# A megakernel's middle stage: a second kind of turn for the chains up to routing, and linear attention's chains at another distance

## The chip, the cores and the metric

The kernel runs on one core of one Trainium2 chip, in one launch. The metric is the device time in microseconds (us) from the first to the last instruction of that core, as a median of several runs. A profiled execution is a further run, with the hardware profiler on; its rows are what the text works with.

## The reference, cut to what matters

Four layers, each an attention and a feed-forward part, follow one another on x of 8 batches x 512 rows x 128 columns in float32. Each part's output is normalised and added to x (the residual). The parts that matter here lie in the middle:

```
L0 attention, L0 mixing                     per batch
L1 attention: a small network learnt step by step over the batches (state handed on from batch to batch),
              then served on each batch
L1 feed-forward: softmax over 8 experts; each row goes to its best expert;
              pos = (cumsum(oh, axis=0) * oh).sum(-1) - 1;  keep = pos < capacity
              y = relu(x @ w1[e] + b1[e]) @ w2[e] + b2[e] for kept rows, x itself for the others
L2 attention: linear attention, softplus of normalised q and k, per batch
L2 feed-forward: every expert picks its best rows over ALL batches, then computes
L3 attention, L3 feed-forward
```

Row positions in the L1 experts are counted over all rows in order, so the batches are routed one after another. The L2 experts choose over all 4096 rows, so they can't begin before the last batch has been through the linear attention and its router.

## The kernel before, in words

The kernel is written with generators. A *chain* is a Python generator that emits some instructions for the engines and then yields; whoever steps the chains sets the order in which instructions stand in the five engines' queues. Each engine works off its own queue in that order.

Stage "first" (L0 attention) is dense and carries the early batches of the other chains in its background. When it ends, `l0` returns the chains that are not finished (`bg.first`). In the built program these are six: `Learn.serve_chain` and `Learn.chain` (at batch 5), `Mix.chain` (batch 6), `Learn.prepare` (batch 6), the residuals of L0 attention (batch 7) and `Route.chain` (the end of batch 4). They are called the *first chains* below: all the work up to routing. The residual of batch 7 feeds mixing of batch 7, that feeds preparing, learning, serving and at last routing of batch 7.

Stage "between" is the stage of this change. An object `Rounds` holds a list of chains, and `turn()` steps every chain once, in the order of the list. Besides the first chains it holds:

- `Passes.chain` (L1 experts). `PASSES = (5, 8)`: pass 1 runs when five batches are routed and takes their rows, pass 2 when all eight are and takes the rows of batches 5 to 7. `once()` runs one pass: four expert inputs are loaded, then a loop over e = 0..9 does `taken(e)` (two transposes on TensorE and a copy on VectorE), `given(e-2)` (16 matmul passes for the second layer, an add on VectorE, a store, and the fetch of a later expert's two weight tiles of 256 KB) and `hidden(e-1)` (8 matmul passes for the first layer, two evictions on ScalarE and two on VectorE), and yields once per e.
- `Pairs.chain`, which adds one `Pairs.batch(b)` per batch: the linear attention chain, with the gather of the L1 experts' results ahead of it and the L2 router behind. It waits until the pass that the batch belongs to is done, adds the chain of a batch, and lets five turns go by before the next (L1256). `Pairs.batch` has 29 steps, most of them one instruction group on one engine: a normalisation is a step of statistics (VectorE, then a power on GpSimd, L194), a step of scaling (ScalarE, four instructions at L217) and a step of adding to x (GpSimd); it has four of them, a query-key-value product (L1311), square, logarithm and exponentials (L1317 to L1339), a product of keys and values (L1342), the output (L1358) and the router (L1399).

`tile_sandwich_kernel` turns the rounds until all eight batches are routed (`route.done`). Then it gives the first chains' memory back and builds `Experts` (the L2 experts), which issues nine loads from SyncE's queue (one of 16 KB that the next line's transposes read, L179, six of 256 KB, two small ones), a further one of 512 KB, and 4 small transposes on TensorE. After that it turns until no chain is left. The stage that follows begins with `l2f_turn_ps` (L1497), which reads the scores of all batches.

A count of the yields gives 92 turns for the stage. Pass 1 is loaded in turn 4 and worked in turns 5 to 14; batch 0 of the linear attention begins in turn 17 and the others at a distance of five turns; routing ends in turn 42; pass 2 is loaded in turn 42 and worked in turns 43 to 52 beside batches 0 to 4; batch 5 begins in turn 54, batch 7 ends in turn 92.

Of the kernel before, what the change touches and what calls it, by code (L numbers as in the profile page):

```python
# [18 lines left out]
B = 8  # L19
# [29 lines left out]
PASSES = (5, B)  # L49
# [21 lines left out]
class Ctx:  # L71


    def __init__(self, es: ExitStack, tc: tile.TileContext, consts: bass.AP):
        self.tc = tc
        nc = self.nc = tc.nc
        pool = lambda name, bufs, **kw: es.enter_context(tc.tile_pool(name=name, bufs=bufs, **kw))
        self.keep = pool("keep", 1)
        self.shared = pool("shared", 2)
        self.dram = pool("dram", 1, space=DRAM)  # L80

        self.c = self.keep.tile([P, C_ALL], F32, name="consts_sb", tag="consts_sb")
        nc.sync.dma_start(self.c, consts)
        self.ident = self.c[:, C_ID : C_ID + P]
        self.triu = self.c[:, C_TRIU : C_TRIU + P]
        self.ones = self.keep.tile([P, P], F32, name="ones", tag="ones")
        nc.vector.memset(self.ones, 1.0)
        self.mhalf = self.keep.tile([P, 8], F32, name="mhalf", tag="mhalf")
        nc.vector.memset(self.mhalf, -0.5)
        self.x = [self.keep.tile([P, NJ, D], F32, name=f"x{b}", tag=f"x{b}") for b in range(B)]  # L90

        self.home = self.keep

        self.ps = pool("ps", 1, space=PSUM)
        self.turn = [0]
        es.enter_context(tc.manual_schedule())

        self.brisk = False
# [154 lines left out]
class Background:  # L253
# [29 lines left out]
    def turn(self, gen):  # L283

        self.first.remove(gen)
        self.first.append(gen)
        self.step(self.first, gen)
# [801 lines left out]
class Passes:  # L1089
# [37 lines left out]
    def once(self, base, rows, results):  # L1127
        cx, nc = self.cx, self.cx.nc
        NF = self.NF
        cap, ns = CAP1, CAP1 // P  # L1130
        of_expert = lambda t, e: t[e * cap : (e + 1) * cap, :].rearrange("(s p) d -> p s d", p=P)
        loads, xts, hts = {}, {}, {}

        def load(e):
            if e < NE:
                loads[e] = cx.work([P, ns, D], "l1f_xg", bufs=4)
                nc.sync.dma_start(loads[e], of_expert(rows, e))

        def taken(e):
            xg = loads.pop(e)  # L1140
            t = cx.bank("l1f_xT_ps")
            for s in range(ns):
                nc.tensor.transpose(t[:, s * P : (s + 1) * P], xg[:, s, :], cx.ident)
            xts[e] = cx.work([D, cap], "l1f_xT")
            nc.vector.tensor_copy(xts[e], t[:, :cap])
            load(e + 4)

        def hidden(e):
            hts[e] = cx.work([P, NF, cap], "l1f_hT")
            xt = xts.pop(e)  # L1150
            for f2 in range(NF // 2):
                hp = cx.bank("l1f_h_ps")
                for i in range(2):
                    f = 2 * f2 + i
                    nc.tensor.matmul(  # L1155
                        hp[:, i * cap : (i + 1) * cap],
                        self.ws[base + e][0][:, f * P : (f + 1) * P],
                        xt,
                        start=True,
                        stop=True,  # L1160
                    )
                for i in range(2):
                    f = 2 * f2 + i
                    src, bias = hp[:, i * cap : (i + 1) * cap], self.b1c[:, f, e : e + 1]
                    if i == 0:
                        nc.scalar.activation(hts[e][:, f, :], src, AF.Relu, bias=bias)
                    else:
                        nc.vector.tensor_scalar(hts[e][:, f, :], src, bias, 0.0, ALU.add, ALU.max)

        def given(e):  # L1170
            ht = hts.pop(e)
            w2 = self.ws.pop(base + e)[1]
            yp = cx.bank("l1f_y_ps")
            for s in range(ns):
                ss = slice(s * P, (s + 1) * P)
                for f in range(NF):
                    nc.tensor.matmul(yp[:, ss], ht[:, f, ss], w2[:, f, :], start=(f == 0), stop=(f == NF - 1))  # L1177
            y = cx.work([P, ns, D], "l1f_y")
            nc.vector.tensor_add(
                y,  # L1180
                yp[:, :cap].rearrange("p (s d) -> p s d", d=D),
                self.b2b[:, e * D : (e + 1) * D].unsqueeze(1).to_broadcast([P, ns, D]),
            )
            nc.sync.dma_start(of_expert(results, e), y)
            self.weights(base + e + 3)

        for e in range(4):
            load(e)
        yield
        for e in range(NE + 2):  # L1190
            if e < NE:
                taken(e)
            if e >= 2:
                given(e - 2)
            if 1 <= e <= NE:
                hidden(e - 1)
            yield


class Rounds:  # L1200


    def __init__(self, chains):
        self.chains = list(chains)

    def add(self, chain):
        self.chains.append(chain)

    def turn(self):
        for chain in list(self.chains):  # L1210
            try:
                next(chain)
            except StopIteration:
                self.chains.remove(chain)


class Pairs:
# [23 lines left out]
    def chain(self, passes, mix, rounds):  # L1241

        cx = self.cx
        for _ in range(3):
            yield
        self.w, self.gw = (
            cx.transposed(w, n, raw=raw) for w, n, raw in zip(self.args, ("w2a", "w2f_gate"), self.raws)
        )
        while not mix.over:
            yield  # L1250
        cx.nc.scalar.preload_act_table_set("natural_log_exp_and_others")
        for b in range(B):
            while passes.done <= self.route.turn(b):
                yield
            rounds.add(self.batch(b))
            for _ in range(5 if b + 1 < B else 0):  # L1256
                yield

    def batch(self, b):
        cx, nc, route = self.cx, self.cx.nc, self.route  # L1260
# [696 lines left out]
@with_exitstack  # L1957
def kernel(ctx: ExitStack, tc: tile.TileContext, a: dict, out: bass.AP):
    cx = Ctx(ctx, tc, a["consts"])
    nc = tc.nc  # L1960
    for b in range(B):
        nc.sync.dma_start(cx.x[b], a["L0_attn_x"][b].rearrange("(j p) d -> p j d", p=P))
    of = lambda layer, *names: [a[f"{layer}_{n}"] for n in names]
    route = Route(cx, *of("L1_ffn", "w_switch", "b_switch"))
    right = ExitStack()
    with cx.phase("first"):
        cx.w = right.enter_context(tc.tile_pool(name="chains", bufs=2, side="right"))
        with cx.beside("attention") as ca:
            mix = Mix(cx, *of("L0_ffn", "W_r", "W_k", "W_v", "mu_r", "mu_k"))
            learn = Learn(cx, route, *of("L1_attn", "t_k", "t_v", "t_q", "W1", "b1", "W2", "b2"))  # L1970
            chains = l0(cx, Attention(ca), *of("L0_attn", "Wq", "Wk", "Wv"), mix, learn)

        cx.brisk = True
        with cx.beside("between") as cb:
            rounds = Rounds(chains)
            passes = Passes(cb, route, *of("L1_ffn", "w1", "b1", "w2", "b2"))
            pairs = Pairs(cb, route, *of("L2_attn", "W_qkv"), *of("L2_ffn", "gate_w"))
            rounds.add(passes.chain())
            rounds.add(pairs.chain(passes, mix, rounds))
            while route.done < B:  # L1980
                rounds.turn()
            right.close()
            ce = right.enter_context(cx.beside("experts", side="right"))
            experts = Experts(ce, pairs, *of("L2_ffn", "ln_w", "ln_b", "fc1s", "b1s", "fc2s", "b2s"))
            while rounds.chains:
                rounds.turn()
    cx.brisk = False
    with cx.phase("last"):
        at = Attention(cx)
        ffn = L3Ffn(cx, *of("L3_ffn", "W1", "b1", "W2", "b2", "Wu", "bu"), out)  # L1990
        with cx.beside("staging") as cs:
            cs.home = cx.home
            weights = l3_weights(cs, *of("L3_attn", "Wqkv", "bqkv", "Wout", "bout"))
            ffn.load()
            weights = experts.run(cs, weights)
        right.close()
        cx.w = right.enter_context(tc.tile_pool(name="tiles", bufs=2, side="right"))
        with right:
            l3(cx, at, experts, ffn, weights)
# [62 lines left out]
```

## Time and profile before

| what | value |
|---|---|
| time, median of 3 runs | 2128.79 us (2126.2 to 2131.81) |
| the profiled execution's own time | 2132.52 us |
| its span, first to last instruction | 2130.7 us |
| TensorE matmul busy over the span | 1772.0 us, 83% |
| VectorE / ScalarE / GpSimd busy | 1290.8 / 1085.9 / 500.2 us |
| granted TensorE clock, mean | 0.871 |
| stage "between": first instruction of turn 1, last of turn 92 | 750.5 us, 1122.8 us |
| routing's scatters to the experts' rows (L1067), 32 of them: first and last start | 347.9 us, 951.1 us |

Busy is the time in which an engine worked on an instruction; a matmul in float32 shows as two records and overlaps its neighbours, so that a busy TensorE is not TensorE at its peak. The granted clock is the share of TensorE's full clock that its throttle let through in the stretch asked for. Idle time of an engine is put down to what ended it.

### The profile page before, as it was taken

The numbers are of one execution on the slowest core, as the hardware profiler recorded it, in microseconds if no ns is written. First come the engines' busy times: TensorE is split into PE (matmuls) and PEld (weight loads), VectorE is DVE, ScalarE is ACT, GpSimd is POOL, SyncE is SP. The second block draws the span as 40 slices with busy tenths as digits, with TensorE's granted clock in tenths as the row PEclk, the third lists the DMA queues.
The fourth block names the chain that finished last, engine by engine and source line by source line (L and its number), as shares of the span: only waits on it lengthen the run. The fifth ranks groups of instructions, "written<-read, shape, count | busy, mean of one in ns | idle before, by whom it ended". The sixth has DMA issues, their size and how long they took to land.

```text
span 2130.7 us, 31833 instructions
## 1 busy us (share of the span) xinstructions
PE 1772.0 (83%) x10886; PEld 1012.4 (48%) x10886; DVE 1290.8 (61%) x4012; ACT 1085.9 (51%) x2272; POOL 500.2 (23%) x566
## 2 busy tenths in 40 slices
PE   3999999898989967649446773799999999999996
PEld 1444545454534456437335552444554454545454
DVE  2777786777777665546447422777666666665522
ACT  1566655555554732346552221366666565665653
POOL 1001111112121122442523485222212121110001
PEclk7999988899988887659565786799999999999998
DMA  5212101011100032016214132111101010100000
GB/s 127 39 33 39 34 16 38 14 39 22 32 16 15 14 104 83 23 27 180 79 50 124 24 42 36 31 32 29 27 9 31 11 27 12 29 12 6 9 6 10
DMA packets 198064, 81.83 MB, mean 38 GB/s; under 512 B 97604, under 2 KB 189674, under 8 KB 197904
## 3 DMA queue, kind: packets, MB, share of 16 engines
q1 hardware_dynamic: 190224, 73.61, 14.3%
q0 software_dynamic: 7680, 6.19, 1.9%
q8 instruction: 87, 1.43, 0.3%
q14 instruction: 73, 0.60, 0.1%
HBM read 45.25 MB, written 31.59 MB: 36 GB/s over the span
## 4 chain that ended last, share of the span: by engine, by line
PE 55%; DVE 23%; ACT 6%; issue 6%; POOL 5%; DMA 3%; SPq 2%; POOLq 0%; ACTq 0%; DVEq 0%
PE at_o L411 11%; PE at_s L393 11%; DVE at_mx L394 8%; PE at_st L400 6%; PE l3f_y_ps L1930 5%; PE l3f_h_ps L1923 5%; DVE ln_st L203 2%; PE flip L239 2%; POOL l2f_out L1686 2%; POOL ln_rs L194 1%; PE l1f_h_ps L1155 1%; PE l1f_y_ps L1177 1%; POOL l2f_xg L1081 1%; PE at_ops L425 1%; DVE ln_mv L205 1%
## 5 line engine op out<-in xcount | busy, mean ns | idle before, releaser
L394 DVE TENSOR_REDUCE at_mx<-at_s 128x1 f32<-128x512 f32 x1024 | 642.3, 681 | 302.3 <-PE at_st L400 233.9
L393 PE MATMUL at_s<-qk 32*128 32x512 f32 x2048 | 612.0, 655 | 35.6 <-DMA qk<-qk_zero 21.3
L403 ACT ACTIVATE at_e<-at_st 128x512 f32<-128x512 f32 x1024 | 535.7, 597 | 193.6 <-PE at_st L400 152.4
L400 PE MATMUL at_st<-qk 32*128 32x512 f32 x2048 | 610.2, 655 | 18.4 <-DVE at_mx L394 12.6
L194 POOL TENSOR_TENSOR ln_rs<-ln_ve,mhalf 128x4 f32<-128x4 f32 x136 | 138.3, 1017 | 837.5 <-DVE ln_ve L188 773.7
L393 PEld LDWEIGHTS at_s<-qk 32*128 32x128 f32 x2048 | 232.2, 194 | 177.4 <-issue 57.7
L400 PEld LDWEIGHTS at_st<-qk 32*128 32x128 f32 x2048 | 240.5, 192 | 111.7 <-issue 41.8
L411 PE MATMUL at_o<-at_e,pad_v 128*32 128x512 f32 x2048 | 254.2, 641 | 14.8 <-DVE at_mx L394 14.8
L411 PEld LDWEIGHTS at_o<-at_e,pad_v 128*32 128x32 f32 x2048 | 66.9, 117 | 197.5 <-issue 173.8
L1930 PEld LDWEIGHTS l3f_y_ps<-w3f,l3f_hT 128*128 128x128 f32 x1024 | 131.8, 197 | 46.3 <-issue 26.8
L1930 PE MATMUL l3f_y_ps<-w3f,l3f_hT 128*128 128x128 f32 x1024 | 136.9, 282 | 3.2 <-ACT l3f_hT L1924 2.0
L419 ACT COPY at_ot<-at_o 128x512 f32<-128x512 f32 x64 | 37.5, 585 | 199.5 <-PE at_o L411 199.5
L1923 PE MATMUL l3f_h_ps<-l3f_xT,w3f 128*128 128x512 f32 x256 | 131.2, 611 | 0.0
L1924 ACT ACTIVATE l3f_hT<-l3f_h_ps,w3f_b1c 128x512 f32<-128x512 f32 x128 | 85.0, 683 | 64.1 <-PE l3f_h_ps L1923 64.0
L1933 DVE SCALAR_TENSOR_TENSOR l3f_o<-l3f_y_ps,l3f_w,l3f_o 128x128 f32<-128x128 f32 x128 | 44.4, 348 | 93.3 <-PE l3f_y_ps L1930 93.1
L217 ACT ACTIVATE l_xn<-x,ln_off,ln_rs 128x128 f32<-128x128 f32 x96 | 39.5, 482 | 81.5 <-DVE ln_off L211 75.4
L239 PE MATMUL flip<-consts_sb,l_xn 128*128 128x128 f32 x96 | 29.6, 398 | 54.4 <-ACT l_xn L217 54.1
L203 DVE BATCH_NORM_STATS2 ln_st<-x 128x6 f32<-128x128 f32 x256 | 55.2, 278 | 18.2 <-POOL x L937 12.4
L1686 POOL DMA_INDIRECT l2f_out<-l2f_y,l2f_idx x32 | 50.5, 1579 | 21.9 <-DVE l2f_y L1683 13.1
L1923 PEld LDWEIGHTS l3f_h_ps<-l3f_xT,w3f 128*128 128x128 f32 x256 | 42.2, 194 | 23.9 <-issue 10.0
L1773 POOL TENSOR_TENSOR l_qk<-l_r,consts_sb 128x256 f32<-128x256 f32 x32 | 21.9, 686 | 133.2 <-DVE l_r L1768 133.2
L366 POOL COPY pad_v<-l_in 128x128 f32<-128x128 f32 x32 | 9.4, 294 | 185.4 <-DMA l_in<-l_v 147.9
(412 smaller groups left out, 2551.0 us busy)
## 6 DMA issues: line engine op xcount, KB each, us to landing
l1f_w<-in_L_ffn_w SPq DMA_DIRECT2D x32, 256.0 KB
l2f_parts<-l2f_out SPq DMA_DIRECT2D x32, 256.0 KB
l2f_out<-l1f_zero SPq DMA_DIRECT2D x24, 256.0 KB
l_qk<-l_qkT SPq DMA_DIRECT2D x16, 256.0 KB
qk<-l_qk SPq DMA_DIRECT2D x128, 32.0 KB
qk<-at_mt SPq DMA_DIRECT2D x256, 2.0 KB
qk<-l_qkT SPq DMA_DIRECT2D x128, 32.0 KB
l2f_x<-l2f_rows SPq DMA_DIRECT2D x8, 272.0 KB
```

The costliest lines, as they stand in the source:

```text
L194: self.nc.gpsimd.tensor_tensor(rs, ve, self.mhalf[:, :NJ], ALU.pow)
L203: nc.vector.bn_stats(st[:, j, :], src[:, j, :])
L239: self.nc.tensor.transpose(t[:, j * P : (j + 1) * P], src[:, j, :], self.ident)
L393: nc.tensor.matmul(s, qk[:, 0, c * P : (c + 1) * P], qk[:, 1, :], start=True, stop=True)
L394: nc.vector.tensor_reduce(mx[n][:, c, h : h + 1], s, AX.X, ALU.max, negate=True)
L400: nc.tensor.matmul(s, qk[:, 1, c * P : (c + 1) * P], qk[:, 0, :], start=True, stop=True)
L403: nc.scalar.activation(es[g][:, h, :], s, AF.Exp, scale=scale)
L411: nc.tensor.matmul(o[32 * h : 32 * h + 32, :], vp[:, c, h, :], e[:, h, :], start=(c == 0), stop=(c == NJ - 1),)
L1686: nc.gpsimd.indirect_dma_start(out=self.pairs.summed[s], out_offset=bass.IndirectOffsetOnAxis(ap=idx[e][:, s : s + 1], axis=0), in_=ys[e][ ...
L1923: nc.tensor.matmul(hp, self.w1[:, e, f * P : (f + 1) * P], xt, start=True, stop=True)
L1924: nc.scalar.activation(hts[e][:, f], hp, AF.Relu, bias=self.b1c[:, f, e : e + 1])
L1930: nc.tensor.matmul(yp[:, :D], hts[e][:, f, js], self.w2[:, e, f, :], start=(f == 0), stop=(f == NF - 1))
```

## The change

Three things are changed in the stage "between".

`Rounds` has two lists, `first` (the first chains) and `chains` (all others). One turn goes through `chains`, and ahead of each of them it steps every chain of `first` once. While there are two others, the first chains thus take two steps in a turn.

`Passes.once` yields three times instead of once after its loads, and, while not all batches are routed, once more between `given` and `hidden`.

`Pairs.chain` lets four turns go by between the chains of batches 0 to 4 and the next, and three after batches 5 and 6, where it was five.

```
-        yield
+        for _ in range(3):
+            yield
         for e in range(NE + 2):
             if e < NE:
                 taken(e)
             if e >= 2:
                 given(e - 2)
+
+            if self.route.done < B:
+                yield
             if 1 <= e <= NE:
                 hidden(e - 1)
             yield
...
-    def __init__(self, chains):
-        self.chains = list(chains)
+    def __init__(self, first):
+        self.first = list(first)
+        self.chains = []
...
+    def step(self, queue, chain):
+        try:
+            next(chain)
+        except StopIteration:
+            queue.remove(chain)
+
     def turn(self):
-        for chain in list(self.chains):
-            try:
-                next(chain)
-            except StopIteration:
-                self.chains.remove(chain)
+        for other in list(self.chains) or [None]:
+            for chain in list(self.first):
+                self.step(self.first, chain)
+            if other is not None:
+                self.step(self.chains, other)
+
+    @property
+    def over(self):
+        return not self.first and not self.chains
...
             rounds.add(self.batch(b))
-            for _ in range(5 if b + 1 < B else 0):
-                yield
+            if b + 1 < B:
+                for _ in range(4 if b < PASSES[0] else 3):
+                    yield
...
-            while rounds.chains:
+            while not rounds.over:
                 rounds.turn()
```

The instructions themselves and their number are those of before; only their order in the queues differs. A count of the yields of the changed kernel gives 80 turns: the first chains take their 42 steps in turns 1 to 21, pass 1 is loaded in turn 4 and worked in turns 7 to 24, `Experts` is built after turn 21, pass 2 is loaded in turn 25 and worked in turns 28 to 37, batches 0 to 7 of the linear attention begin in turns 26, 30, 34, 38, 42, 46, 49 and 52, and batch 7 ends in turn 80.

## The prediction

> **What bounds the kernel now.** I read three views of the profile: the busy time by stretch, the waits by stretch, and the page's costliest groups. The change touches nothing outside the stage "between" (750.5 to 1122.8 us, 372.3 us of a span of 2130.7), so that stage alone is priced. Its stretches are turns 1 to 16 (pass 1), 17 to 41 (first chains and batches 0 to 4), the pause around the last scatter, turns 43 to 52 (pass 2 with batches 0 to 4) and turns 53 to 92 (the other batches):
>
> ```profile
> 750.00:842.00 92.00, 65.73 (x412) 56.55 (x412) 52.27 (x205) 27.52 (x63) 20.41 (x24) 0.85 0.36 105
> 842.00:951.00 109.00, 65.69 (x242) 47.21 (x241) 57.90 (x292) 44.66 (x100) 52.44 (x49) 0.61 0.07 21
> 951.00:960.00 9.00, 1.34 (x8) 1.35 (x9) 5.14 (x25) 2.11 (x5) 4.07 (x4) 0.50 0.42 123
> 960.00:1010.00 50.00, 46.10 (x297) 40.00 (x295) 32.32 (x139) 33.14 (x74) 10.88 (x10) 0.98 0.58 172
> 1010.00:1123.00 113.00, 55.51 (x185) 36.93 (x184) 52.27 (x281) 61.23 (x135) 44.07 (x41) 0.59 0.27 76
> ```
>
> The columns are length, TensorE, its weight loads, VectorE, ScalarE, GpSimd (each with its count), granted clock, DMA share, GB/s. Only 960 to 1010 has a full engine (TensorE, 46 of 50 us). Elsewhere no engine is over 75% busy: the time is latency, handed from engine to engine. The waits say so, here VectorE, ScalarE and GpSimd waiting for each other in the last stretch (total us, times, longest):
>
> ```profile
> POOL ln_rs L194 <- DVE ln_ve L188: 36.7, 11, 6.0
> ACT l_xn L217 <- DVE ln_off L211: 17.8, 7, 4.7
> DVE l2a_m L1347 <- PE l2a_kv_ps L1342: 16.8, 4, 4.8
> ```
>
> In the late part of pass 1 (798 to 842) TensorE's queue stands for a first chain's VectorE work, with the expert's matmuls queued behind it; and at 951 it stands for a load that `Experts` issues:
>
> ```profile
> PE l0f_k_ps L668 <- DVE ln_off L211: 7.2, 1, 7.2
> ...
> PE col L179 <- DMA raw_b<-in_L_ffn_b1s: 8.1, 1, 8.1
> ```
>
> **How I price turns.** The steps of a turn fall to different chains, so they can run side by side as far as engines differ. For each turn I add up, engine by engine, the measured durations of the steps in it, and take the fullest engine; summed over turns this is a floor that only overlap across turns can undercut. Against the present trace the floor is 49.0 us for turns 43 to 52 (took 50.3, factor 1.03, five batches and a pass in flight), 34.5 for turns 17 to 26 (took 32.0 with ScalarE's last piece, factor 0.93), 31.6 for turns 35 to 41 (took 40.7, factor 1.29) and 100.6 for turns 53 to 92 (took 113.1, factor 1.12, mostly two to four batches in flight). The main durations, from the page and from the view of one tile:
>
> ```profile
> L194 POOL TENSOR_TENSOR ln_rs<-ln_ve,mhalf 128x4 f32<-128x4 f32 x136 | 138.3, 1017 | 837.5 <-DVE ln_ve L188 773.7
> L203 DVE BATCH_NORM_STATS2 ln_st<-x 128x6 f32<-128x128 f32 x256 | 55.2, 278 | 18.2 <-POOL x L937 12.4
> L217 ACT ACTIVATE l_xn<-x,ln_off,ln_rs 128x128 f32<-128x128 f32 x96 | 39.5, 482 | 81.5 <-DVE ln_off L211 75.4
> L1317 ACT ACTIVATE l2a_sq<-l2a_qkv x8: 1056/1060/1062, 891.2 to 1084.8; 128x1024 f32<-128x1024 f32 x8
> ```
>
> One batch's 29 steps add to 17.3 us of ScalarE (20 scalings at 482 ns are 9.6 of them), 16.2 of VectorE (16 statistics at 278 ns are 4.4) and about 19 of TensorE.
>
> **Part 1, the first chains take two steps a turn: gains time.** They have 42 steps. Now these cost 750.5 to 951 less what the pass and the batches add. (a) Steps 1 to 8 took 39 us (750.5 to 789.6), with three full expert steps in them, of some 1.5 us each on the path: 35 without. (b) Steps 9 to 16 took 52.9 us with experts at every turn; the first chains' own floor in them is 29 us, times about 1.1: 32. (c) Steps 17 to 42 were cheapest at 842 to 871 us, where three or four first chains and hardly a batch ran: TensorE and VectorE ended turns 17 to 26 at 871, 29 us for 10 steps, 2.9 each, so 26 x 2.9 = 75. Sum 142, where now 200.5 pass until the last scatter's issue.
>
> **Part 2, experts in two pieces.** The same matmuls, 4.3 us per expert at full clock (1.89 us first layer, 1.95 second, 0.42 transposes, measured at 780 to 788 us). Each piece of about 2 us stands alternately beside a whole round of first chains, and the first layer no longer stands in TensorE's queue directly behind its own transposes and the copy on VectorE. I cost the pieces inside the rounds at nothing, because a round of 2.9 us whose chains wait for VectorE covers 2 us of TensorE; without that cover the 12 pieces of turns 9 to 20 cost about 24 us. What is left of pass 1 after routing (turns 22 to 24: 1.89 + 3.84 + 1.95 us of TensorE, the eviction and a store) is bare: 8 us.
>
> **Part 3, `Experts` moves from turn 42 to turn 21.** Its ten loads go to SyncE's queue right after the last scatter. Its four transposes wait for one of them on TensorE, 8.1 us today and no less then; behind them stand pass 1's last pieces and so pass 2. Take 8 us. Besides, in the present order pass 2's first four loads stand ahead of Experts' loads; in the new one they and pass 1's last two stores stand behind them: 6 x 256 KB + 512 KB = 2.0 MB, at the 172 GB/s of 960 to 1010 us 12 us. They start some 2.5 us before TensorE goes on (first such load at 957.0, transposes done at 959.3), and 8 us more are pass 1's bare tail; I add 2 (bounds 0, if the queue's loads run side by side, and 12). The gathers of batch 0 read what those stores write and come later still.
>
> So the stretch up to pass 2 lasts 142 + 8 + 8 + 2 = 160 us. Turn 26 then begins near 750.5 + 160 = 910.5; the corresponding point is now 959.5. Gain 49 us.
>
> **Part 4, all linear attention comes after routing: loses time.** At 959.5 us batches 0 to 4 have today done 26, 21, 16, 11 and 6 steps: 80 of 232. In the new order none has begun at 910.5, because `passes.done` becomes 1 only in turn 25. So 232 steps are left with pass 2, against 152 with pass 2 now. The new turns, by the floor and its factor:
> - turns 26 and 27: a load and little else, 4 us.
> - turns 28 to 37: pass 2 with one to three batches; TensorE is fullest with 4.3 us a turn; floor 39.5, times 1.03: 40.7.
> - turns 38 to 46, four to five batches: 29.3 x 1.03 = 30.2.
> - turns 47 to 62, six to eight batches: floor 85.2 (ScalarE alone 62.3, VectorE 55; they peak in different turns, for example 7.3 us of ScalarE in turn 52, 6.7 of VectorE in turn 54) x 1.03 = 87.8.
> - turns 63 to 80, five batches down to one: 53.9 x 1.12 = 60.4.
>
> Sum 223 us, against 163 now: a loss of 60. The distance of four and three turns instead of five is within these sums. A step that waits here holds its engine's queue for the batches behind it; what helps is that a gather's landing (2.2 to 4.1 us, twice on the chain of waits at 1025 and 1043 us) is hidden in turns of 4 us and more. SyncE's queue carries five stores and loads per batch as before, nothing waits on them but the next stage's gathers.
>
> **Sum.** 750.5 + 160 + 223 = 1133.5 against 1122.8: +11 us. The profiled execution's own time, 2132.5 (its span and 1.8 us around it), becomes 2143.5; it lay 3.7 us over the median of the runs, so I put 2128.8 + 11 = **2140 us**. Own range 2126 to 2154.
>
> [...] The row first: where pass 2 ran beside the batches the clock was 0.98 and a key-value matmul took 286 ns; without a pass it was 0.59 and the same took 418 ns (medians of both stretches).
>
> ```profile
> L1342 PE MATMUL l2a_kv_ps<-l2a_qkv x16: 286/286/331, 970.5 to 998.6; 128*128 128x144 f32 x16
> ...
> L1342 PE MATMUL l2a_kv_ps<-l2a_qkv x32: 286/418/610, 1015.3 to 1100.8; 128*128 128x144 f32 x32
> ```
>
> My TensorE durations are of the slow stretch already. [...]
>
> **The rivals.**
> - *The engines fill* (not slower). With six to eight batches in flight nothing has to wait inside a turn, and turns run into each other. From ScalarE's total, turns 47 to 62 take 62 us, not 88. For it: turns 17 to 26 undercut the floor (0.93). Against it: queues in program order, and 1.29 in turns 35 to 41 with five batches in flight. Then +11 - 25.5 = -14.5: 2114 us. It decides if those turns take under 4.5 us each.
> - *The rounds don't shorten* (slower). If pass pieces and first chains still hold each other in TensorE's queue, (c) costs halfway from 2.9 to the 5.0 us a step of turns 1 to 5, 3.95, so 26 x 1.05 = 27 more: 2167 us. It decides if the last scatter is issued after 906 us. For it: turns 11 to 16 at 7 us each. Against it: these had whole experts.
> - *It cancels* (no change): factor 1 throughout, 2129 us.
>
> **How the numbers follow.** Forecast 0.48, engines fill 0.27, rounds don't shorten 0.20, cancels 0.05. The uncertainty of a comparison is about 0.3%, 6.4 us. Of the forecast's 0.48, 0.05 falls below 2122, 0.10 within 6.4 us, 0.33 above. With the others: faster 0.05 + 0.25 = 0.30; same 0.10 + 0.02 + 0.05 = 0.17; slower 0.33 + 0.20 = 0.53. The range leaves out the ends of both rivals, 0.1 each: 2108 to 2168.
>
> **What would show it.** Last scatter issued at 888 to 900 us (it is 951.1 now); first gather near 918 (844.9 now); pass 2 with TensorE full at 914 to 955; turns of about 5.5 us from 985 to 1073, ScalarE and VectorE near 70% at a clock of about 0.6; `l2f_turn_ps` at 1130 to 1137 (1122.9 now). I am wrong if the batches' turns with seven in flight take 4 us, or if routing ends late; and if a buffer that eight batches in flight share (three of `l2_o`) makes a queue stand.

## The result and the profile after

| | before | changed |
|---|---|---|
| median of the runs | 2129.82 us (2123.37 to 2133.85, 6 runs) | 2144.1 us (2142.85 to 2147.01, 6 runs) |
| profiled execution, span | 2130.7 us | 2141.1 us |
| last scatter of routing starts | 951.1 us | 915.6 us |
| pass 2's first transpose | 959.2 us | 937.6 us |
| first and last gather of the linear attention's batches | 844.9, 1058.5 us | 940.4, 1048.7 us |
| `l2f_turn_ps`, the end of the stage | 1122.9 us | 1137.0 us |
| from there to the end | 1007.8 us | 1004.1 us |

The ratio is 1.0071 with a 95% interval of 1.0054 to 1.0089: slower by 14 us. Routing ends 35 us earlier, pass 2 begins 22 us earlier, and the stage ends 14 us later.

First the busy time by stretch of the changed kernel, with the columns of the prediction (length, TensorE, weight loads, VectorE, ScalarE, GpSimd, granted clock, DMA share, GB/s). The cuts are turns 1 to 4, 5 to 8, two for turns 9 to 21, the pause up to pass 2, pass 2 (turns 28 to 37), turns 38 to 46, 47 to 62 and 63 to 80:

```profile
750.00:782.00 32.00, 15.61 (x88) 12.71 (x89) 20.94 (x89) 7.88 (x18) 12.31 (x16) 0.73 0.33 95
782.00:825.00 43.00, 29.68 (x121) 22.09 (x121) 19.99 (x88) 12.87 (x29) 8.13 (x10) 0.57 0.04 11
825.00:895.00 70.00, 48.72 (x254) 40.23 (x254) 37.24 (x150) 17.46 (x42) 12.65 (x12) 0.77 0.17 48
895.00:921.00 26.00, 13.34 (x68) 11.60 (x67) 5.38 (x24) 1.88 (x5) 3.93 (x4) 0.70 0.26 68
921.00:936.00 15.00, 10.47 (x51) 8.47 (x50) 2.98 (x7) 1.89 (x4) 0.00 (x0) 0.84 0.73 223
936.00:976.00 40.00, 38.14 (x219) 32.29 (x220) 18.57 (x68) 14.02 (x31) 15.84 (x15) 0.93 0.53 151
976.00:1002.00 26.00, 16.32 (x47) 9.31 (x45) 15.55 (x80) 18.67 (x39) 16.93 (x17) 0.74 0.15 40
1002.00:1082.00 80.00, 49.15 (x169) 32.70 (x169) 53.75 (x267) 57.63 (x128) 42.64 (x40) 0.70 0.21 59
1082.00:1137.00 55.00, 32.25 (x129) 24.76 (x129) 30.11 (x171) 35.44 (x83) 18.17 (x17) 0.62 0.41 116
```

Three things are to be seen. In 782 to 825 the experts are hardly there (121 matmuls), and yet four turns take 43 us with no engine over 70%. Pass 2 is a stretch of full TensorE of 40 us. In 1002 to 1082 ScalarE is busy 57.63 of 80 us, 72%, where the end of the stage had 54% before (61.23 of 113).

The waits of the same three places, in order (total us, times, longest): the first chains at 782 to 825, the pause at 895 to 936, the full turns at 1002 to 1082.

```profile
PE l0f_k_ps L668 <- DVE ln_off L211: 7.3, 1, 7.3
...
PE col L179 <- DMA raw_b<-in_L_ffn_b1s: 10.6, 1, 10.6
...
POOL ln_rs L194 <- DVE ln_ve L188: 18.3, 8, 5.7
ACT l_xn L217 <- DVE ln_off L211: 13.6, 6, 5.2
```

The first line stood in the profile of before too, with 7.2 us; it is the same wait, though no expert is beside it now. TensorE waits 10.6 us for `Experts`' small load (8.1 before). GpSimd's waits for VectorE, 36.7 of the 113 us from 1010 to 1123 of before (32%), are 18.3 of the 80 us from 1002 to 1082 (23%).

Behind that load stands the rest of pass 1, and behind its stores stand pass 2's inputs, as SyncE's own order of issue shows (start, length, line, transfer):

```profile
918.77 0.33 SPq L167 DMA_DIRECT2D raw_b<-in_L_ffn_b1s  x1
...
927.91 0.38 SPq L1184 DMA_DIRECT2D l1f_given<-l1f_y  x1
...
932.10 0.38 SPq L1184 DMA_DIRECT2D l1f_given<-l1f_y  x1
...
933.53 2.03 SPq L1137 DMA_DIRECT2D l1f_xg<-l1f_taken  x4
```

The two stores at L1184 are pass 1's last results. Pass 2's four inputs (L1137) are issued at 933.5, 18 us after the last scatter.

### The profile page after: what moved, and what is told of

Its sections match the earlier page's. It is cut to its first block, busy times and chain, and to the rows that moved or that the text cites. A ratio compares the mean times of both kernels' runs of the same rounds, so it can differ in the third digit from the quotient of the medians.

```text
span 2141.1 us, 31864 instructions
## 1 busy us (share of the span) xinstructions
PE 1786.4 (83%) x10886; PEld 1021.8 (48%) x10886; DVE 1294.1 (60%) x4012; ACT 1086.1 (51%) x2272; POOL 498.8 (23%) x566
## 4 chain that ended last, share of the span: by engine, by line
PE 34%; DVE 11%; ACT 5%; issue 4%; POOL 3%; DMA 2%; SPq 0%; POOLq 0%; ACTq 0%; DVEq 0%
PE at_s L393 6%; PE at_o L411 5%; PE l3f_y_ps L1947 5%; PE l3f_h_ps L1940 5%; PE at_st L400 3%; DVE at_mx L394 3%; POOL l2f_out L1703 2%; PE flip L239 1%; PE l1f_y_ps L1177 1%; DVE ln_st L203 1%; PE l1f_h_ps L1155 1%; POOL l2f_xg L1081 1%; ACT l_xn L217 1%; PE l_qkv_ps L1783 1%; DVE l2f_junk L1523 1%
## 5 line engine op out<-in xcount | busy, mean ns | idle before, releaser
L1067 POOL DMA_INDIRECT l1f_taken<-l1f_xn,l1f_place x32 | 32.1, 1003 | 113.9 <-DMA l1f_taken<-l1f_xn,l1f_place 26.3
```

## The experiments

The change has three parts: double turns (the first chains take two steps a turn), the split (experts in two pieces, three yields after the loads), and the closer distance (four and three). All eight combinations were timed, the changed kernel and the kernel before among them. Each ratio is to the kernel before in runs on the same chip; its median was 2129.8 us beside the changed kernel and 2128.8, 2129.0 and 2133.3 us in the three groups of further runs, so ratios are compared, not medians.

| double turns | split | distance | turns | median, us | ratio, 95% interval |
|---|---|---|---|---|---|
| no | no | five | 92 | | 1 |
| no | no | four, three | 88 | 2111.7 | 0.9925 [0.9901, 0.9950] |
| no | yes | five | 92 | 2140.7 | 1.0049 [1.0031, 1.0067] |
| no | yes | four, three | 88 | 2133.0 | 1.0002 [0.9989, 1.0015] |
| yes | no | five | 79 | 2180.3 | 1.0212 [1.0187, 1.0237] |
| yes | no | four, three | 70 | 2135.2 | 1.0040 [1.0019, 1.0061] |
| yes | yes | five | 89 | 2184.9 | 1.0261 [1.0234, 1.0288] |
| yes | yes | four, three (the change) | 80 | 2144.1 | 1.0071 [1.0054, 1.0089] |

The marks of the stage in each run's profile, one execution each, in us from the span's start:

| run | last scatter | pass 2's first transpose | `l2f_turn_ps` |
|---|---|---|---|
| closer distance alone | 946.8 | 955.1 | 1109.0 |
| the change at distance five | 918.8 | 940.6 | 1178.1 |
| the change with whole experts | 924.3 | 937.9 | 1132.6 |
| pass 1 after routing | 907.3 | 962.9 | 1160.7 |
| split alone | 939.9 | 947.4 | 1131.7 |
| distances three and two | 953.2 | 961.2 | 1102.6 |
| closer distance, later `Experts` | 945.2 | 949.5 | 1111.0 |
| the change, later `Experts` | 918.2 | 929.6 | 1129.9 |
| double turns alone | 927.8 | 940.7 | 1173.6 |
| split and closer distance | 938.0 | 947.5 | 1126.1 |
| distances two and one | 956.6 | 964.9 | 1101.1 |
| pass 1 after routing, added matmuls | 896.8 | 953.5 | 1155.4 |

**Closer distance alone.** The kernel before with one hunk of the change:

```
-            for _ in range(5 if b + 1 < B else 0):
-                yield
+            if b + 1 < B:
+                for _ in range(4 if b < PASSES[0] else 3):
+                    yield
```

> The kernel before with the distances of four and three turns alone; 88 turns instead of 92, batches still begin in turn 17. If the late turns are latency (my theory: turns of the last stretch take about 3 us whether two or four batches are in flight), four turns fewer save 8 to 12 us, ratio 0.994 to 0.996. If engines were full there, or queues stand for each other more with more in flight, the same work takes the same time: ratio 0.999 to 1.003.

2111.7 us, 0.9925 [0.9901, 0.9950], somewhat more than the 8 to 12 us of the first expectation. This one hunk makes the kernel 16 us faster; so the other two parts lose about 30. The stage ends at 1109.0 instead of 1122.9, most of it won behind the start of pass 2: from its first transpose to `l2f_turn_ps` pass 153.9 us, in the kernel before 163.7. There the work is also less: by a count of the yields 90 of the 232 batch steps are done when routing ends, where it was 80, and routing ends no later for it.

**The change at distance five.** The same hunk reversed in the changed kernel.

> The changed kernel with the old distance of five turns: 89 turns instead of 80, all batches still after routing. If turns are latency, nine turns more cost 9 x 2.5 to 3 us less what thinner turns save, some 10 to 20 us over the changed kernel: 2154 to 2164. If the engines' totals decide, it comes out within 5 us of the changed kernel's 2144.

2184.9 us, 1.0261 [1.0234, 1.0288], 20 us over the first expectation and far from the second: both missed. The first chains end near where they do in the changed kernel (918.8 against 915.6), but the stage ends 41 us later, 38 of them behind the start of pass 2. Here is that stretch at distance five, and then the same stretch of the changed kernel:

```profile
976.00:1178.00 202.00, 114.58 (x359) 75.52 (x358) 99.22 (x530) 115.75 (x256) 82.87 (x77) 0.59 0.22 62
```

```profile
976.00:1137.00 161.00, 97.72 (x344) 66.77 (x342) 99.42 (x516) 111.75 (x249) 77.74 (x74) 0.68 0.27 75
```

In both kernels all 232 batch steps are left when routing ends. The work is almost the same (VectorE 99.22 and 99.42 us, ScalarE 115.75 and 111.75), the time is not: ScalarE is 57% busy in one and 69% in the other. What the closer distance buys here is fewer gaps. TensorE is busy longer at distance five, at a granted clock of 0.59 instead of 0.68.

**The change with whole experts.** The changed kernel without the split:

```
-        for _ in range(3):
-            yield
+        yield
...
-            if self.route.done < B:
-                yield
```

> The changed kernel with whole experts and one yield after their loads: first chains still step ahead of each other chain; pass 1 ends in turn 15, batches begin in turn 16 and routing ends in turn 19; 70 turns. Theory 'start': the split's price is that batch 0 waits for the end of routing, so that 232 batch steps come after it; here some begin before, and pass 1 is done earlier, so 10 to 30 us under the changed kernel: 2115 to 2135. Theory 'rounds': whole experts hold the first chains up in TensorE's queue and win back nothing: 2140 to 2155.

2135.2 us, 1.0040 [1.0019, 1.0061], between the two expected ranges, at the edge of the first. Whole experts stretch the first chains by 8.7 us (924.3), although routing ends in turn 19 instead of 21 (a batch that already runs adds a third step to their turns), yet pass 1 ends earlier, pass 2 begins at the same time (937.9), and the stage ends 4.4 us sooner. The split is on the slower side in all four pairs of the table, by 0.3% to 0.8%; under double turns the intervals of the pairs overlap a little.

**Pass 1 after routing.** In the changed kernel `Passes.chain` waits until all eight batches are routed, so that the first chains run by themselves:

```
-            while route.done < n:
+            while route.done < B:
                 yield
```

> The changed kernel with pass 1 held back until all batches are routed, so that the first chains run with nothing beside them: the price of their 42 steps by themselves. If the pieces of pass 1 cost the rounds something, the last scatter is issued well before the 915.6 us of the changed kernel (892 by the forecast's 142 us). If the steps are pure latency at a low TensorE clock, it is issued at 905 to 925 all the same, with a granted clock near 0.55. The whole run is some 30 to 40 us longer than the changed kernel, since pass 1 then stands bare.

2167.8 us in one execution, 24 us over the changed kernel where 30 to 40 were expected; the last scatter, at 907.3, lies in the range of pure latency. From the first matmul of the stage (L887) to the last scatter pass 156.1 us (751.2 to 907.3), in the changed kernel 165.0 (750.6 to 915.6). The pass's pieces therefore cost the first chains 9 us; done in the open, between 921.2 and 957.7, the same pass takes 36.5. The pieces are well hidden, and 156 us are the first chains' own. The stretches of this run:

```profile
782.00:825.00 43.00, 29.71 (x120) 22.19 (x118) 19.57 (x86) 12.73 (x30) 8.59 (x9) 0.56 0.03 8
825.00:870.00 45.00, 30.96 (x120) 24.45 (x119) 23.05 (x101) 9.58 (x23) 5.40 (x5) 0.52 0.02 7
870.00:907.00 37.00, 10.49 (x42) 8.75 (x42) 10.03 (x51) 4.68 (x11) 10.22 (x10) 0.50 0.03 10
```

782 to 825 is what it is in the changed kernel, with 120 matmuls against 121. In the last 37 us every engine is under 30% busy. They hold the last batch's serving, with batch 6's scatters beside it, and then its routing; the chain of waits ends in its four scatters, of which each waits until the one before has landed (GpSimd's three waits for a landing add to 5.7 us; start, length, what):

```profile
898.60 2.20 DMA l1f_taken<-l1f_xn,l1f_place
...
901.55 2.12 DMA l1f_taken<-l1f_xn,l1f_place
...
904.42 2.14 DMA l1f_taken<-l1f_xn,l1f_place
```

They follow each other at 2.9 us, and in this run hardly anything is left to run beside them.

**Split alone.** The kernel before with the split of the experts, one yield after the loads:

```
+            if self.route.done < B:
+                yield
             if 1 <= e <= NE:
                 hidden(e - 1)
```

> The kernel before with one part of the change only: experts in two pieces until all is routed (a yield between given and hidden); one step a turn, distance five as before. Turns stay 92, batch 0 of the linear attention begins in turn 26 instead of 17. Theory (the double turns are what costs the +2.6% of the change without the closer distance, the split by itself only moves batch 0 later into the pass-2 stretch): 2128 to 2140 us, +0.2% as a middle. Rival (the split costs most of it, by keeping linear attention out of the rounds of the first chains): over 2150 us, with the last scatter earlier than 951 us and the stretch after it longer than 185 us.

2140.7 us, 1.0049: 0.7 us over the theory's range and far from the rival's time, though with the rival's two signs. The last scatter comes 11.2 us earlier (939.9), and from there to `l2f_turn_ps` 191.8 us pass instead of 171.8. Batch 0 begins nine turns later, and by a count of the yields 38 batch steps are done when routing ends, where it was 80: the rest is done behind it.

**Distances three and two** in the kernel before, as a difference to the closer distance alone:

```
-                for _ in range(4 if b < PASSES[0] else 3):
+                for _ in range(3 if b < PASSES[0] else 2):
```

> The kernel before with distances three and two instead of five (the change has four and three); 86 turns. Theory (the stage is latency of turns with few chains; a closer distance fills them and takes turns away from the end): four and three gave 2111.7; two turns fewer at the end at 2.5 to 3 us each and fuller turns before: 2103 us, 2097 to 2109. Rival (fuller turns get longer by what the end saves): 2110 to 2118 us.

2108.6 us, 0.9898 [0.9878, 0.9918]: inside the theory's range, and faster than both kernels. The intervals of this and of four and three overlap, so the further 3 us are not settled. Of the batch steps 100 are done when routing ends, and that comes only 2 us later than in the kernel before (953.2 against 951.1).

**Closer distance and later `Experts`**: four and three in the kernel before, and

```
             while route.done < B:
                 rounds.turn()
+            for _ in range(4):
+                rounds.turn()
             right.close()
```

> The kernel before with distances four and three, and Experts built four turns later than the last routing, when pass 2's inputs are loaded and its matmuls stand ahead. Theory (TensorE's wait of 8 to 10 us for Experts' small load is on the path, because pass 2 stands behind it): 6 to 9 us under 2111.7, so 2103 to 2106. Rival (pass 2 can't begin sooner anyway, as its own inputs land only after the last scatter): 2109 to 2114, with pass 2's first transposes within 2 us of 955.1.

2119.3 us, 0.9947 [0.9927, 0.9967]: both expectations missed, and no gain on the closer distance alone. Pass 2 does begin 5.6 us sooner (949.5), but it ends at 1005.2, where it ended at 1004.6. TensorE now stands for the same load in the middle of pass 2, here at 965 to 985:

```profile
PE col L179 <- DMA raw_b<-in_L_ffn_b1s: 4.6, 1, 4.6
```

The wait was moved, not removed; in 970 to 980 TensorE is busy 5.45 us, where it was 9.97 with the closer distance alone.

**The change with later `Experts`**: the same hunk with five turns, in the changed kernel.

> The changed kernel, with Experts built five turns after the last routing (turn 26 instead of 21). Theory (the 10.6 us that TensorE waited there holds pass 1's rest and with it pass 2): pass 2's first transposes move from 937.6 to 928 to 931 us, and the time from 2144.1 to 2135 to 2138. Rival (the loads' place in the queue decides nothing, or the pause moves into pass 2): 2142 to 2146.

2140.2 us, 1.0046 [1.0031, 1.0060]. Pass 2 begins at 929.6, as the theory has it, and the stage ends 7.1 us sooner (1129.9), but the time lies between both expectations, 4 us under the change, and the intervals of the two ratios overlap. TensorE's wait for the small load is not gone:

```profile
PE col L179 <- DMA raw_b<-in_L_ffn_b1s: 7.9, 1, 7.9
```

It ends at 929.1, right ahead of pass 2's transposes, where pass 2's inputs are on their way anyway: they are issued at 923.1 instead of 933.5, because pass 1's rest and its stores now stand ahead of the wait. So the place of the wait decides what it costs. In the profiled execution the rest of the kernel takes 1011.1 us instead of 1004.1; a rest of 1011.0 us is also in the profile of the run with added matmuls, where `Experts` stands as in the change. That the move lengthens the rest is thus not shown.

**Double turns alone**: the changed kernel without the split (as above) and at distance five.

> The kernel before with one part of the change only: the first chains take two steps a turn while two others are there; experts whole, one yield after the loads, distance five. 80 turns. Theory (two steps a turn take the linear attention out of the rounds before routing, so its batches run behind with few in flight, and only a closer distance brings that back): the closer distance is worth 25 to 40 us here as it was with the split, so 2135 + 25 to 40 = 2160 to 2175 us. Rival (the parts add up; the closer distance is worth the 17 us that it brings on the kernel before): 2148 to 2156 us.

2180.3 us, 1.0212 [1.0187, 1.0237]. As a time that is over both ranges, but on this chip the kernel before took 2133.3 us; at 2128.8 us, from which the ranges were reckoned, the ratio gives 2174, the upper end of the theory's. The theory holds: under double turns the closer distance takes 1.7% off (1.0212 to 1.0040), under single turns 0.75%. The double turns are the part that costs: last scatter 23 us earlier, end of the stage 51 us later. When routing ends, 4 batch steps are done instead of 80.

**Split and closer distance**, one step a turn:

> The kernel before with the split experts and the distance of four and three, one step a turn; 88 turns. Theory (the split costs 12 us whatever the distance, the closer distance brings 17): 2121 to 2127 us. Rival (with a batch 0 that begins nine turns later, a closer distance is worth more): under 2118 us.

1.0002 [0.9989, 1.0015]: both expectations missed. Beside the split the closer distance brings 0.5%, 10 us, and not 16, a difference that is within the intervals. That the parts don't simply add is shown by the double turns, under which the distance brings 1.7% and 1.9%.

**Distances two and one** in the kernel before, as a difference to the closer distance alone:

```
-                for _ in range(4 if b < PASSES[0] else 3):
+                for _ in range(2 if b < PASSES[0] else 1):
```

> The kernel before with distances two and one; 84 turns. Theory (what shortens the stage is fewer turns at its end): two turns of 2 to 2.5 us less than with three and two, 2102 to 2106 us. Rival (the turns fill up, and fewer of them cost as much): 2107 to 2114 us.

2109.9 us, 0.9885 [0.9864, 0.9905]. By the ratio it can't be told from three and two (0.9898); at 2128.8 us for the kernel before it would be 2104 us, in the theory's range. The stage speaks for the rival: from its first matmul (L887, at 752.9 us with three and two, 751.4 here) to `l2f_turn_ps` pass 349.7 us in both profiles, two turns fewer and nothing gained. Either of the two is the best version found, 1.0% to 1.2% under the kernel before and, by the quotient of the ratios, 1.7% to 1.8% under the changed one.

Under single turns the gain goes with the steps that a closer distance moves ahead of the end of routing. At five, at four and three, at three and two, and at two and one 80, 90, 100 and 110 of the 232 batch steps are done by then, and from the last scatter to `l2f_turn_ps` pass 171.8, 162.2, 149.4 and 144.5 us, while the last scatter itself stays between 946.8 and 956.6. No run separates this from the turns that it saves at the end. Under double turns next to no step can move, and the gain is in the gaps.

**Pass 1 after routing, with added matmuls.** After each step of a first chain TensorE gets a matmul of 128x128 that nothing reads:

```
+            t = self.cx.bank("warm")
             for chain in list(self.first):
                 self.step(self.first, chain)
+                self.cx.nc.tensor.matmul(t[:, :P], self.cx.ident, self.cx.ident, start=True, stop=True)
```

> The changed kernel with pass 1 held until all is routed (as in the run of the first chains alone, last scatter 907.3 us, clock 0.56 at 782 to 825 and 0.52 at 825 to 870), and a matmul of 128x128 whose result nobody reads after every step of a first chain, so that TensorE has no long idle window. Theory (the low clock lengthens the first chains' rounds once the experts are out of them): clock over 0.8 in both stretches, the steps of 782 to 825 take 33 to 37 us instead of 43, last scatter at 885 to 895 us. Rival (the rounds are latency on other engines): last scatter at 904 to 915 us whatever the clock.

2168.2 us in one execution (2167.8 without them). The clock rose, in 782 to 825 from 0.56 to 0.80 and in 825 to 870 from 0.52 to 0.79:

```profile
782.00:825.00 43.00, 34.96 (x211) 28.68 (x211) 20.86 (x93) 12.29 (x27) 8.57 (x10) 0.80 0.03 9
825.00:870.00 45.00, 33.81 (x203) 28.94 (x202) 23.88 (x103) 7.42 (x18) 7.27 (x7) 0.79 0.03 8
```

And the matmuls became short: those that learn's step uses (L887), first in the run without the added matmuls, then with them (minimum, median, maximum in ns over the stage):

```profile
L887 PE MATMUL l1a_g_ps<-l1a_e,l1a_c x24: 272/421/423, 751.2 to 852.7; 128*32 128x128 f32 x24
```

```profile
L887 PE MATMUL l1a_g_ps<-l1a_e,l1a_c x24: 272/273/297, 743.0 to 844.1; 128*32 128x128 f32 x24
```

The last scatter at 896.8 looks like a gain of 10 us, but this execution also entered the stage 8 us sooner, at 743.0. From there to the last scatter pass 153.8 us, against 156.1. (Since the stage begins 8 us sooner, the two stretches above hold somewhat later steps in this run than in the run without the added matmuls.) So the higher clock brings some 2 us, net of what the added matmuls take themselves (91 more records in 782 to 825, 5 us of TensorE). As a mark 896.8 is in neither expected range; reckoned from the entry the rival holds: these rounds are latency, and the clock was low where TensorE had fewer matmuls (0.56 with 120 records in 782 to 825, 0.80 with 211).

## Why the prediction was right

The time was right: 2140 us forecast, 2144.1 measured, a stage of +14 instead of +11 us. The direction rests on a mechanism that the runs bear out: the first chains gain, and the batches, taken out of their rounds, lose more behind routing (the double turns alone: 23 us won, 51 us later at the end). That the sum came within 4 us is luck: two errors of some 22 us and opposite sign cancelled. Of its own signs the last scatter (888 to 900 us) and the first gather (918) were missed, at 915.6 and 940.4, and "if routing ends late" stood among its signs of being wrong; the end of the stage (1130 to 1137) was met at 1137.0.

*The first chains, 142 us forecast, 165 measured.* (a) Steps 1 to 8 took 32 us (35). (b) Steps 9 to 16 took 43 (32), and (c) steps 17 to 42 took 90.6, 3.5 each (75, 2.9 each). What failed in (b) is the factor of 1.1 on the first chains' floor. It took the time above the floor for the experts' matmuls, queued behind a first chain's wait at L668; that wait is 7.3 us with no expert beside it, and with hardly anything else in flight the steps take about 1.5 times their floor (43 over 29), with pass 1 after routing too. That the second step of a chain in a turn waits for its first would explain it, but no run shows that by itself. In (c) the price of 2.9 a step came from 842 to 871 us, where three or four first chains were in flight; towards the end one is, and its scatters follow at 2.9 us each by themselves. With pass 1 after routing (c) takes 82 us: 7 of the 16 us too many are the first chains' own, and some 9 are the pass's pieces, which part 2 cost at nothing.

*The pause.* From the last scatter to turn 26 I put 18 us (bare tail 8, `Experts` 8, order of the queue 2); it took about 20 (915.6 to 936). The wait itself was 10.6. The order of SyncE's queue did hold pass 2's inputs, not by bytes, but because pass 1's last stores stand ahead of them and wait for TensorE: its last second-layer matmuls (L1177) ended at 931.6 us, the last store was issued at 932.1 and the inputs at 933.5. Moving `Experts` shortened the way from the last scatter to pass 2 from 22.0 to 11.4 us, though a wait of 7.9 us stayed in it.

*The batches behind routing, 223 us forecast, 201 measured.* Turns 28 to 37 took 38.4 us (40.7), 38 to 46 25.8 (30.2), 47 to 62 80 (87.8), 63 to 80 55 (60.4). The terms that were mis-sized are the factors on the floors, 1.03 and 1.12 by the trace of before; they are 0.97, 0.88, 0.94 and 1.02 here. Turns run into each other, most of all those with four and more batches in flight. That is the mechanism of the rival "the engines fill", at a third of its size: its turns of under 4.5 us were not reached, they took 5.0.

*Rivals.* "The rounds don't shorten" had its condition fulfilled (last scatter after 906), but not its time, since the other term paid 22 us back. Nor was its price reached by its mechanism: it put 27 us on (c) for pieces and first chains that hold each other up; (c) cost 16 more, 9 of them by the pieces. Routing ends 35 us earlier, and the gain went into the 232 batch steps that were left, where it had been 152.

*The distance.* "Within these sums" was true, since the turns were counted with it, but the sum hid that the change holds parts of opposite sign: the distance is worth 0.75% by itself and 1.9% inside the change, and the other two together cost 2.6%. Parts priced one by one would have set the one that gains apart from the two that lose.

*The clock.* The prediction's row gives 0.59 and 418 ns for a key-value matmul in 1010 to 1123 of the kernel before. In the changed kernel the granted clock was 0.70 in 1002 to 1082 and 0.62 in 1082 to 1137, and the same matmul took 447 ns (median of 1002 to 1137):

```profile
L1359 PE MATMUL l2a_kv_ps<-l2a_qkv x56: 286/447/610, 1002.8 to 1110.3; 128*128 128x144 f32 x56
```

The turns came out shorter than by my rows all the same: 80 us where 87.8 were put down, and 55 where it was 60.4. Where the first chains ran alone the clock was 0.50 to 0.56.

What stays open: why steps 9 to 16 take half as much again as their floor; whether the rest of the kernel, 1004 to 1011 us in the profiles, depends on where `Experts` is built; and whether three and two or two and one is the better distance.

## What to carry to other kernels

In this stage, which is bound by latency, the time went by how many independent chains are in flight and by how much of their work is done beside other chains: the change that speeds one dependent chain by taking the others out of its rounds only moved their work to where fewer are left to cover it. In such a stage try chains that start closer together before anything is reordered. Price each part of a compound change by itself, because the good part can be hidden in a small sum.

## What the runs showed of the hardware

Without the experts' matmuls in the rounds the granted clock was 0.56 (782 to 825 of the run with pass 1 after routing, 120 matmuls), where the kernel before had 0.89 (204), and a float32 matmul of 128 columns (L887) went from 273 to 421 ns (medians over the stage); some 91 extra matmul records brought it back to 0.80 and 273 ns and were worth some 2 of 156 us. The low clock went here with fewer matmuls, and little of the time hung on it. And from the end of the stage on, where the instructions are the same in every kernel, profiled executions differ by up to 7 us (1004.1 to 1011.1), so that a few microseconds of a stage are read from the stage's own marks and not from one time.
